# Where a pair's copies out of PSUM stand in the order of a two-layer graph attention kernel

## The chip, the cores and the metric

The kernel runs on one core of a Trainium2 chip. The metric is device time in microseconds (us), the median of several runs; lower is better. Times inside an execution come from one profiled execution.

## What is computed

Two graph attention layers over a batch of 8 graphs with 2048 nodes and 256 features, each followed by a residual add and a layer norm. Layer 0 has 8 heads of 32 features and additive scores; layer 1 has one head and scores from a product.

```python
def _L0_gnn_ref(x, adj, prior, W, a_src, a_dst, beta_tilde, W_out):
    x_proj = jnp.einsum('bnd,hdf->bhnf', x, W)
    e_src = jnp.einsum('bhnf,hf->bhn', x_proj, a_src)
    e_dst = jnp.einsum('bhnf,hf->bhn', x_proj, a_dst)
    e = jax.nn.leaky_relu(e_src[..., :, None] + e_dst[..., None, :], ALPHA)
    e = e + (beta * jnp.log(prior + EPS))[:, None, :, :]
    e = jnp.where(adj[None, None, :, :] > 0, e, neg_inf)
    attn = jax.nn.softmax(e, axis=-1)
    h = jnp.einsum('bhij,bhjf->bhif', attn, x_proj)
    return h.transpose(0, 2, 1, 3).reshape(B, N, D) @ W_out.T
...
def _L1_gnn_ref(inp, adj, W1, W2, W3):
    h1, h2, h3 = inp @ W1, inp @ W2, inp @ W3
    e = jax.nn.leaky_relu(jnp.einsum('bnd,bmd->bnm', h1, h2), ALPHA)
    e = jnp.where(adj[None, :, :] > 0, e, NEG_INF)
    return jax.nn.relu(softmax(e) @ h3)
...
x = _layernorm(x + _L0_gnn_ref(x, adj, adj[None], ...), axis=-1)
x = _layernorm(x + _L1_gnn_ref(x, adj, ...), axis=-1)
```

## The kernel before

**Layer 0** is the class `Gat`, one object per batch. It works on pairs of heads (four pairs, 0 to 3) and on 16 column tiles of 128 nodes per pair; one call of `step` does one tile of one pair, 64 steps per batch. VectorE (DVE) makes two score tiles `s` of 128x2048 (L381, from `c`, `re` and the matrix `mt` loaded from memory; the ring of such tiles has eight). TensorE (PE) multiplies them into two PSUM accumulators, `val` (the weighted sums) and `den` (the denominators), both 128x1024 and with one buffer each (L414). From batch 1 on, for pairs 1 to 3, half or so of the denominators' terms are added up beforehand in two tiles `d`: the first term by ScalarE (ACT, L399), the others by DVE (L394); at the end of the pair one product of `d` with ones adds them into `den`.

When the last tile of a pair is done, `finish` empties the accumulators on ACT: two copies of half of `val` each into `ht` (L429) and one of `den` into `dn` (L431). `finish` is a generator: its further stages, one per later step, are a small load `rc` from `dn`, a reciprocal on DVE (L436), a round trip through memory (`rec_d`, `rb`) and the scaling of `ht` (L457).

**Layer 1** is the class `Dot`, which works on the batch before. One call of its `step` does one row tile of 128 nodes: for each of four column blocks, PE transposes a block of the last row tile's probabilities `p` into a PSUM tile `pt` (L580), ACT copies it to `pts` (L582), PE makes the next row tile's scores `e` for that block (L554) and ACT writes them to `p` (L556). Then PE multiplies `pts` into `acc` (L596), DVE masks the new `p` and takes its extreme (L559, `neg`), ACT takes the exponential (L562), scales `acc` into `z` (L601), and DVE (`z` L602, `st` L226, `mv` L228) and ACT (`f` L230 to L233, `z` L234) normalise the row tile. Every fourth row tile PE first makes new queries `h` (L543), copied by ACT (L545). All the PSUM tiles `pt`, `e`, `h1p` and the like rotate through three buffers of one tag (`mm`).

**The order.** The main loop puts a few steps of layer 0 of batch b between the row tiles of layer 1 of batch b-1. The last step of each pair comes at the end of such a group, so a row tile of `Dot` follows it (after pair 0: the end of `turn` and the start of `Dot`). PE's order, and from the main loop on SP's too, is the order in which the code is written. On the other engines a scheduler orders the instructions, with the order of writing as the priority; each engine then executes its instructions in that fixed order. The generators of finished pairs are kept in the list `later`, which all batches share, and each step of layer 0 advances each of them once.

Of the kernel before, what the change touches and what calls it, by code (L numbers as in the profile page):

```python
# [27 lines left out]
def kernel(  # L28
# [51 lines left out]
    def mm_tile(name):  # L80
        return ps.tile([P, BK], F32, tag="mm", name=name)

    def ring_tile(name, shape=(P, N)):


        return wide.tile(list(shape), F32, tag="s", name=name, bufs=8)

    def wide_tile(name, tag, bufs, dtype=F32):
        return wide.tile([P, N], dtype, tag=tag, name=name, bufs=bufs)
# [116 lines left out]
    def load_mt(jt, tag="mt"):  # L206
        mt = wide_tile("mt", tag, 2)
        nc.sync.dma_start(mt, mt_d[ts(jt, P), :])
        return mt
# [13 lines left out]
    def layer_norm(z):  # L223

        st = small.tile([P, nc.vector.BN_STATS_DIM], F32, name="st", bufs=2)
        nc.vector.bn_stats(st, z)  # L226
        mv = small.tile([P, nc.vector.BN_AGGR_DIM], F32, name="mv", bufs=3)
        nc.vector.bn_aggr(mv, st)  # L228
        f = small.tile([P, 4], F32, name="f", bufs=3)
        nc.scalar.activation(f[:, 0:1], mv[:, 1:2], AF.Ln, bias=eps_ln)  # L230
        nc.scalar.activation(f[:, 1:2], f[:, 0:1], AF.Exp, scale=-0.5)
        nc.scalar.mul(f[:, 2:3], mv[:, 0:1], -1.0)
        nc.scalar.activation(f[:, 3:4], f[:, 1:2], AF.Identity, scale=f[:, 2:3])  # L233
        nc.scalar.activation(z, z, AF.Identity, bias=f[:, 3:4], scale=f[:, 1:2])  # L234

    def row_tile(name, bufs=4):
        return small.tile([P, D], F32, tag="row", name=name, bufs=bufs)


    class Gat:  # L240

# [104 lines left out]
        def step(self, count=1):  # L346

            for _ in range(count):
                hp, jt = next(self.units)
                for work in list(self.later):  # L350
                    if next(work, self) is self:
                        self.later.remove(work)
                if hp == NP - 1 and jt == 0 and self.b + 1 < B:
                    gats[self.b + 1].load_factors()

                at = self.b * NP + hp + 1
                if at < B * NP:
                    gat = gats[at // NP]
                    if jt == 4 and gat.b > 0:
                        gat.load(at % NP)  # L360
                    elif jt == 12:
                        gat.scale(at % NP)
                if jt == 0:
                    if self.b > 0:
                        self.cs = [self.cs_ahead.pop(0) for _ in range(HP)]
                    else:
                        self.cs = [self.query_rows(hp * HP + a) for a in range(HP)]
                    self.val = pacc.tile([P, HALF], F32, tag="val", name="val")
                    self.den = pacc.tile([P, HALF], F32, tag="den", name="den")
                first = self.b == 0 and hp == 0  # L370
                if first:
                    self.more_mt(jt + 2, jt > 0)
                if self.b > 0:
                    mt = self.mts.pop(0)
                else:
                    mt = self.mts[jt] if first else load_mt(jt, ("mt", "d")[jt % 2])
                s = []
                for a in range(HP):
                    h = hp * HP + a
                    sa = ring_tile("s")  # L380
                    nc.vector.scalar_tensor_tensor(sa, self.cs[a], self.re[:, 0, jt, h:h + 1], mt, ALU.max, ALU.mult)  # L381
                    s.append(sa)
                    if self.b > 0 and jt == NT - 1:
                        self.cs_ahead += [c for c in [next(self.c_loads, None)] if c]
                if self.b > 0:
                    ahead = 2 if hp > 0 or not 1 < jt < 10 else min(4, 11 - jt)
                    while len(self.mts) < ahead and (mt := next(self.mt_loads, None)):
                        self.mts.append(mt)
                v, e = self.v[hp], self.re[:, 1]
                heads = [hp * HP + a for a in range(HP)]  # L390
                chain = SUMMED[self.b][hp]
                if jt - 1 in chain[1:]:
                    for d, sa, h in zip(self.sums, self.last, heads):
                        nc.vector.scalar_tensor_tensor(d, sa, e[:, jt - 1, h:h + 1], d, ALU.mult, ALU.add)  # L394
                self.last = s
                if jt in chain[:1]:
                    self.sums = [wide_tile("d", "d", 2) for _ in heads]
                    for d, sa, h in zip(self.sums, s, heads):
                        nc.scalar.activation(d, sa, AF.Copy, scale=e[:, jt, h:h + 1])  # L399
                self.products(self.val, [v[:, jt, ts(a, DH)] for a in range(HP)], s, jt == 0, jt == NT - 1)  # L400
                if jt not in chain:
                    self.products(self.den, [e[:, jt, h:h + 1].to_broadcast([P, DH]) for h in heads], s,
                                  jt == min(set(range(NT)) - set(chain)), not chain and jt == NT - 1)
                if chain and jt == NT - 1:
                    self.products(self.den, [ones] * HP, self.sums, False, True)
                if jt == NT - 1:
                    work = self.finish(hp)
                    next(work)
                    self.later.append(work)

        def products(self, dst, weights, s, start, stop):
            for c in range(HALF // BK):
# [116 lines left out]
    class Dot:  # L529
# [35 lines left out]
        def step(self, fill=lambda k: None):  # L565

            it, p, den = self.at, self.p, self.ahead
            self.at += 1  # L570
            xr = row_tile("x1r")
            nc.sync.dma_start(xr, x1_d[self.b, ts(it, P), :])
            fill(0)

            pts = []

            def turned(g):
                t = mm_tile("pt")
                for k in range(IG):
                    nc.tensor.transpose(t[:, ts(k, P)], p[:, ts(g * IG + k, P)], ident)  # L580
                pt = chunk.tile([P, BK], F32, tag="pt", name="pts", bufs=NB)
                nc.scalar.copy(pt, t)  # L582
                pts.append(pt)

            if it + 1 < NT:
                if (it + 1) % IG == 0:
                    self.queries((it + 1) // IG)
                self.scores(it + 1, turned)
            else:
                for g in range(NB):  # L590
                    turned(g)
            acc = pacc.tile([P, D], F32, tag="acc", name="acc")
            for g in range(NB):
                for k in range(IG):
                    j = g * IG + k
                    nc.tensor.matmul(acc, pts[g][:, ts(k, P)], self.h3[:, j, :], start=(j == 0), stop=(j == NT - 1))  # L596
            fill(1)
            rec = small.tile([P, 1], F32, name="rec1", bufs=2)
            nc.vector.reciprocal(rec, den)
            z = row_tile("z")  # L600
            nc.scalar.activation(z, acc, AF.Relu, scale=rec)  # L601
            nc.vector.tensor_add(z, z, xr)  # L602
            layer_norm(z)
            nc.scalar.dma_start(out[self.b, ts(it, P), :], z)
# [79 lines left out]
    for b in range(1, B + 1):  # L684
        gat, fresh = gats[b - 1], gats[b] if b < B else None
# [71 lines left out]
```

## Time and profile before

| | |
|---|---|
| median of 3 runs | 4280.19 us (4280.04 to 4282.62) |
| the profiled execution | 4279.62 us |
| its span, first to last instruction | 4277.8 us |
| mean granted TensorE clock | 0.997 |
| ACT copies `ht<-val` (L429) | 64, 1.01 us each |
| ACT copies `dn<-den` (L431) | 32, 1.01 us each |
| ACT copies `pts<-pt` (L582) | 512, 0.585 us each |
| ACT `d<-s,re` (L399) | about 2.0 us each |
| DVE `s` (L381) | 1024, 2.34 us each |
| DVE idle for `p` from ACT (L559 after L556) | 254.4 us, 29 times |

A group of the timeline is one row: its start from the start of the span, how long it took from first start to last end, engine, line, operation, the tiles written and read, how many instructions; in brackets the engine's idle time before it and what ended that. An instruction's end overlaps the start of the next one on its engine by about a tenth of a microsecond, so start-to-start distances are what adds up.

### The profile page before, as it was taken

The numbers are of one execution on the slowest core, as the hardware profiler recorded it, in microseconds if no ns is written. First come the engines' busy times: TensorE is split into PE (matmuls) and PEld (weight loads), VectorE is DVE, ScalarE is ACT, GpSimd is POOL, SyncE is SP. The second block draws the span as 40 slices with busy tenths as digits, with TensorE's granted clock in tenths as the row PEclk, the third lists the DMA queues.
The fourth block names the chain that finished last, engine by engine and source line by source line (L and its number), as shares of the span: only waits on it lengthen the run. The fifth ranks groups of instructions, "written<-read, shape, count | busy, mean of one in ns | idle before, by whom it ended". The sixth has DMA issues, their size and how long they took to land.

```text
span 4277.8 us, 59110 instructions
## 1 busy us (share of the span) xinstructions
PE 4163.8 (97%) x24928; PEld 2230.3 (52%) x24928; DVE 3618.3 (85%) x2432; ACT 1609.0 (38%) x3007; POOL 10.3 (0%) x14
## 2 busy tenths in 40 slices
PE   7999999999999999999999999999999999999999
PEld 4444355555555555554555555555545555555766
DVE  6888778998899979999799988999799997998222
ACT  6522133333334333342333323333333323343554
POOL 0000000000000000000000000000000000000000
PEclk9999999999999999999999999999999999999999
DMA  7988656657455555555555474556555565553211
GB/s 239 309 287 321 242 210 219 231 203 247 184 201 192 197 205 188 184 196 214 187 208 185 174 248 153 209 187 210 198 191 182 181 233 182 205 182 134 77 49 41
DMA packets 268458, 843.52 MB, mean 197 GB/s; under 512 B 33184, under 2 KB 166304, under 8 KB 194464
## 3 DMA queue, kind: packets, MB, share of 16 engines
q1 hardware_dynamic: 232352, 806.17, 53.2%
q10 hardware_dynamic: 35840, 33.57, 2.3%
q8 instruction: 195, 3.19, 0.3%
q14 instruction: 71, 0.58, 0.0%
HBM read 763.76 MB, written 75.37 MB: 196 GB/s over the span
## 4 chain that ended last, share of the span: by engine, by line
PE 57%; DVE 27%; issue 8%; DMA 5%; ACT 3%; SPq 0%; DVEq 0%; ACTq 0%; POOL 0%; POOLq 0%
DVE s L381 17%; PE acc L596 13%; PE e L554 12%; PE val L414 11%; PE den L414 9%; DVE d L394 6%; PE pt L580 3%; PE h3p L522 2%; DMA mt<-mt_d 2%; PE proj L274 2%; DVE p L559 2%; PE y L483 2%; PE h1p L543 2%; DMA adj_r<-in_adj_dram 1%; DMA adj_t<-in_adj_dram 1%
## 5 line engine op out<-in xcount | busy, mean ns | idle before, releaser
L381 DVE SCALAR_TENSOR_TENSOR s<-c,re,mt 128x2048 f32<-128x2048 f32 x1024 | 2357.5, 2340 | 195.4 <-PE den L414 59.7
L414 PE MATMUL val<-s,v 128*32 128x512 f32 x8192 | 978.8, 597 | 22.0 <-DVE s L381 21.9
L554 PE MATMUL e<-x1t,h 128*128 128x512 f32 x2048 | 964.6, 595 | 21.6 <-ACT pts L582 18.5
L596 PE MATMUL acc<-h,pts 128*128 128x256 f32 x4096 | 905.0, 379 | 0.0
L596 PEld LDWEIGHTS acc<-h,pts 128*128 128x128 f32 x4096 | 777.8, 190 | 156.4 <-issue 57.4
L414 PE MATMUL den<-s,re 128*32 128x512 f32 x5600 | 683.4, 593 | 0.0
L394 DVE SCALAR_TENSOR_TENSOR d<-s,re,d 128x2048 f32<-128x2048 f32 x282 | 654.0, 2343 | 0.0
L414 PEld LDWEIGHTS val<-s,v 128*32 128x32 f32 x8192 | 252.3, 110 | 599.0 <-issue 530.7
L559 DVE CUSTOM_DVE_ANT_0 p<-p,pen 128x2048 f32<-128x2048 f32 x128 | 292.5, 2285 | 260.5 <-ACT p L556 254.4
L554 PEld LDWEIGHTS e<-x1t,h 128*128 128x128 f32 x2048 | 351.2, 190 | 287.6 <-issue 249.8
L556 ACT ACTIVATE p<-e 128x512 f32<-128x512 f32 x512 | 305.2, 596 | 416.9 <-PE e L554 414.3
L562 ACT ACTIVATE p<-p,neg 128x2048 f32<-128x2048 f32 x128 | 256.5, 2004 | 472.2 <-DVE neg L559 472.2
L414 PEld LDWEIGHTS den<-s,re 128*32 128x32 f32 x5600 | 188.9, 110 | 418.8 <-issue 418.8
L580 PEld LDWEIGHTS pt<-ident,p 128*128 128x128 f32 x2048 | 245.2, 141 | 301.5 <-issue 237.5
L582 ACT COPY pts<-pt 128x512 f32<-128x512 f32 x512 | 297.0, 585 | 228.9 <-PE pt L580 226.2
L580 PE MATMUL pt<-ident,p 128*128 128x128 f32 x2048 | 309.8, 276 | 16.0 <-ACT p L562 8.3
L230 ACT ACTIVATE f<-mv,eps_ln 128x1 f32<-128x1 f32 x128 | 37.9, 296 | 434.8 <-DVE mv L228 434.2
L601 ACT ACTIVATE z<-acc,rec 128x256 f32<-128x256 f32 x128 | 60.0, 469 | 250.7 <-PE acc L596 102.4
L274 PE MATMUL proj<-wp,xt 128*128 128x272 f32 (+1 forms) x512 | 130.7, 400 | 4.7 <-ACT xt L182 3.0
L522 PE MATMUL h3p<-w3s,x1t 128*128 128x256 f32 x512 | 122.6, 383 | 6.4 <-ACT x1t L517 4.7
L483 PE MATMUL y<-wot,ht 128*128 128x256 f32 x512 | 119.0, 385 | 3.5 <-ACT x1t L517 2.1
L276 ACT COPY v<-proj 128x256 f32<-128x256 f32 x128 | 47.2, 374 | 197.2 <-PE proj L274 153.7
(88 smaller groups left out, 1895.4 us busy)
## 6 DMA issues: line engine op xcount, KB each, us to landing
mt<-mt_d SPq DMA_DIRECT2D x496, 1024.0 KB
c<-c_d SPq DMA_DIRECT2D x64, 1024.0 KB
pen<-pen_d SPq DMA_DIRECT2D x112, 512.0 KB
xg<-in_x_dram SPq DMA_DIRECT2D x60, 512.0 KB
adj_t<-in_adj_dram SPq DMA_DIRECT2D x16, 1024.0 KB
mt_d<-mt SPq DMA_DIRECT2D x16, 1024.0 KB
rb<-rec_d SPq DMA_DIRECT2D x128, 128.0 KB
x_d<-ht ACTq DMA_DIRECT2D x64, 256.0 KB
```

What stands on the lines that cost most here:

```text
L274: nc.tensor.matmul(t[:, 0:cols], xt[kc][:, ts(it % IG, P)], wp[:, kc, 0:cols], start=(kc == 0), stop=(kc == KC - 1))
L381: nc.vector.scalar_tensor_tensor(sa, self.cs[a], self.re[:, 0, jt, h:h + 1], mt, ALU.max, ALU.mult)
L394: nc.vector.scalar_tensor_tensor(d, sa, e[:, jt - 1, h:h + 1], d, ALU.mult, ALU.add)
L414: nc.tensor.matmul(dst[ts(q, DH), ts(c, BK)], weights[q % 2], s[q % 2][:, ds(q // 2 * HALF + c * BK, BK)], start=start, stop=stop)
L522: nc.tensor.matmul(t[:, ts(i, D)], x1t[:, kc, ts(2 * (j - lag) + i, P)], w3s[:, kc, :], start=(kc == 0), stop=(kc == KC - 1))
L554: nc.tensor.matmul(t, self.h1[:, kc, ts(it % IG, P)], self.x1t[:, kc, ts(c, BK)], start=(kc == 0), stop=(kc == KC - 1))
L556: nc.scalar.activation(p[:, ts(c, BK)], t, AF.Prelu, alpha=ALPHA)
L559: nc.vector.tensor_tensor_reduce(p, p, pen, -1.0, FMAX, ALU.add, ALU.min, neg)
L562: nc.scalar.activation(p, p, AF.Exp, bias=neg, scale=-1.0, accum_out=den)
L580: nc.tensor.transpose(t[:, ts(k, P)], p[:, ts(g * IG + k, P)], ident)
L582: nc.scalar.copy(pt, t)
L596: nc.tensor.matmul(acc, pts[g][:, ts(k, P)], self.h3[:, j, :], start=(j == 0), stop=(j == NT - 1))
```

## The change

At the end of a pair the generator `finish` is no longer advanced at once to its copies. It goes into a list `evictions`. The function `evict` takes what is in that list, issues the copies, and puts the generator into `later`. It is called at the beginning of each step of layer 0, and in layer 1's row tile after the next row tile's scores have been written and before the product `acc`. For batch 0 it is called right at the pair's end.

```diff
+    evictions = []
+
+    def evict():
+
+        while evictions:
+            gat, work = evictions.pop()
+            next(work)
+            gat.later.append(work)
...
         def step(self, count=1):

             for _ in range(count):
+                evict()
                 hp, jt = next(self.units)
                 for work in list(self.later):
...
                 if jt == NT - 1:
-                    work = self.finish(hp)
-                    next(work)
-                    self.later.append(work)
+                    evictions.append((self, self.finish(hp)))
+                    if self.b == 0:
+                        evict()
...
             else:
                 for g in range(NB):
                     turned(g)
+            evict()
             acc = pacc.tile([P, D], F32, tag="acc", name="acc")
```

## The prediction

> **What bounds the kernel now.** I read the page's engine table first, then who waited for whom on PE, then the timeline of PE, ACT and DVE at the ends of the pairs, and the DVE waits in the stretches between them.
>
> ```profile
> PE 4163.8 (97%) x24928; PEld 2230.3 (52%) x24928; DVE 3618.3 (85%) x2432; ACT 1609.0 (38%) x3007; POOL 10.3 (0%) x14
> ...
> PE val L414 <- DVE s L381: 21.9, 17, 4.4
> PE e L554 <- ACT pts L582: 18.5, 24, 1.9
> PE pt L580 <- ACT p L556: 5.7, 12, 0.8
> PE e L554 <- ACT h L545: 3.1, 6, 0.7
> ```
>
> PE is busy for all but 114 us of 4277.8, so this change cannot win much: only PE's gaps are for sale. The second wait line is the one that the change aims at: 24 times the e product waited for ACT's copy of a transposed tile, 18.5 us in all. 15.3 us of it stand at the ends of pair 1 and pair 2 of batches 1 to 7, one each, found by going through the timeline there. Here is one pair 1 end (batch 3), PE and then ACT (start, duration, instruction, in brackets the idle time before it):
>
> ```profile
> 1706.33 1.88 PE L554 MATMUL e<-x1t,h 128*128 128x512 f32 x4
> 1708.05 0.60 PE L580 MATMUL pt<-ident,p 128*128 128x128 f32 x4
> 1709.79 1.99 PE L554 MATMUL e<-x1t,h 128*128 128x512 f32 x4 [1.14 <-ACT pts L582]
> ...
> 1714.18 0.66 PE L580 MATMUL pt<-ident,p 128*128 128x128 f32 x4 [0.26 <-ACT p L556]
> ...
> 1706.35 2.01 ACT L399 ACTIVATE d<-s,re 128x2048 f32<-128x2048 f32 x1 [1.83 <-DVE s L381]
> 1708.26 0.99 ACT L431 COPY dn<-den 128x1024 f32<-128x1024 f32 x1
> 1709.15 0.58 ACT L582 COPY pts<-pt 128x512 f32<-128x512 f32 x1
> ```
>
> The score tiles use three PSUM buffers, so the second e product needs the buffer of the first pt, and that is free only when ACT has copied it. ACT stands in 1.9 us of d (start to start) and 0.9 us of dn before it. The same at the end of pair 2:
>
> ```profile
> 1837.73 1.98 PE L554 MATMUL e<-x1t,h 128*128 128x512 f32 x4 [0.89 <-ACT pts L582]
> ...
> 1834.15 2.00 ACT L399 ACTIVATE d<-s,re 128x2048 f32<-128x2048 f32 x1 [1.39 <-PE den L414]
> 1836.18 1.01 ACT L431 COPY dn<-den 128x1024 f32<-128x1024 f32 x1
> 1837.09 0.59 ACT L582 COPY pts<-pt 128x512 f32<-128x512 f32 x1
> ```
>
> Pair 0 and pair 3 ends show no such gap. One more thing limits the gain: asked for DVE's waits between 1597 and 1830, the trace names none, and the table by stretches (columns: length, busy PE, PEld, DVE, ACT, POOL, clock, DMA share, GB/s) has DVE at 100% there, while PE still runs almost without gaps:
>
> ```profile
> 1604.00:1704.00 100.00, 98.95 (x583) 52.18 (x582) 100.00 (x62) 31.45 (x58) 0.00 (x0) 1.00 0.50 180
> 1704.00:1724.00 20.00, 18.60 (x86) 11.15 (x90) 20.00 (x16) 12.82 (x20) 0.00 (x0) 1.00 0.77 285
> 1724.00:1834.00 110.00, 109.55 (x664) 56.25 (x656) 107.30 (x72) 37.68 (x74) 0.00 (x0) 1.00 0.51 181
> ```
>
> So in pairs 1 and 2 DVE and PE are level, and PE time won at the end of pair 1 is kept only as far as DVE delivers.
>
> **What the Trainium skill says.** "PSUM — Partial Sum Buffer", section "Engine vs sequencer instructions": the queues of ScalarE and VectorE are strict FIFO. The trace agrees: pt was ready at 1706.99 and its copy waited 2.16 us behind d and dn. "Perfetto Trace Analysis", section "Optimizing Scalar/DVE Operations": an unsaturated Scalar engine can still cause bubbles on other engines. ACT is at 38% here and makes this one. The same page, section "Identifying the Most-Contended Engine", warns that PE's busy share is no measure of distance from its limit; I use only PE's gaps, 98 us between its matmuls (the rest of the 114 is ahead of the first). The prices below are all from the trace.
>
> **The change part by part.** No instruction is added or removed. In the changed program PE's order and SP's and POOL's queues are the same as before, DMAs included. Batch 0 evicts at once as before. What moves, by the order in which the built programs hold their instructions:
>
> (a) ACT, pairs 1 and 2: the two val copies and the first d stay ahead of the first pts copy; dn goes behind the second pts copy. Pair 1, replayed with the start-to-start times above: d 1706.35, pts 1708.26 (done 1708.84), p 1708.74, pts 1709.23, two small f 1709.71, dn 1710.0, p 1711.0. The second e starts at about 1708.9 instead of 1709.79: 0.89 won, 0.25 of the gap stays. p at 1711.0 instead of 1713.54 also ends the 0.26 gap before the last pt, because the second d now stands behind it. Pair 1: 1.15 us.
>
> (b) Pair 2: pts 1836.08, p 1836.57, pts 1837.05, dn 1837.53, d 1838.43, p 1840.33. The second e starts on time (the 0.89 gap goes). But the last pt needs the buffer that this p empties at 1840.93, and now wants it at about 1840.6: a new gap of some 0.35, where before the 0.89 gap had hidden it. After it the next pts copy, 1841.4, is just in time. Net about 0.6 to 0.7 us.
>
> (c) DVE between the ends of pair 1 and pair 2: the scheduler puts p (L559) one s (2.26 us) earlier twice, and one d earlier once, and mv (L228) of one tile ahead of one d. Before, that mv (1779.45) held ACT's f/z chain and the h copy behind it, and PE waited 0.45 us at 1781.74. In the new order mv is some 1.8 us earlier, so this gap goes as well, even with PE 1.15 us earlier. Against it: at 1716.1 DVE now meets p at the head of its queue; ACT finishes writing it at about 1716.55, so DVE idles some 0.45 us in a stretch without slack. At its other early places p has been written 0.8 us before or more.
>
> (d) What is late next: the s of the last row tile of pair 2. Before, it ended at 1827.83 and PE's val product began at 1828.77, 0.93 later (in batches 2 to 7 alike). In the new order z, st and one rec stand behind it (about 0.8 us less), plus 0.45 idle: 1827.5. PE may then start at 1827.5 at the earliest, so of the 1.6 us won in (a) and (c) some 1.3 are kept.
>
> (e) Pair 0: dn moves from before the x1t copy to between the two h copies. ACT had 1.13 us idle before the second h, dn takes 0.9: hidden; without that cover it would cost at most 0.9. The h and dn tiles also swap places in a ring of four; both take places of xg tiles long read. Pair 3: one f between the val copies. Nothing.
>
> (f) rc's load waits for dn, now about 1 to 2 us later. SP is in order, so the mt and rb loads behind it could start later. DVE's rc (L436) comes at 1716.10, 6.9 us after dn's end, so I take nothing; the bounds are 0 and 1 us per end. The den product that overwrites the PSUM of dn comes 15 us later.
>
> Batch 1: its pair 1 gap (1.87 us) ends with pts held by an f that waits for mv at 708.2, and stays; its pair 2 is as (b), but DVE there waits for DMA. I take 0.5 us.
>
> Sum: six batches (2 to 7) by 1.3 + 0.65 = 11.7, plus 0.5: 12.2 us. The profiled execution took 4279.62 us (span 4277.8 and 1.8 around it), 0.57 below the median of 4280.19. 4280.19 - 12.2 is about 4268.
>
> **The rivals.**
> Both ends in full: no cap in (d), no new gap in (b): 6 x (1.40 + 0.45 + 0.89) + 0.5 = 17 us, 4263. For it: the replay's margins are tenths. Against it: DVE at 100%.
> DVE swallows pair 1: only (b) stays, 6 x 0.65 + 0.5 = 4.4, 4276. It happens if DVE loses about 1.3 us more than replayed. For it: no DVE idle time before; against: the new order itself gives 0.8 back.
> The stall only moves: dn, wherever it stands on ACT, delays a p or pts copy that PE needs, the gaps keep their sum, 4280. Against it: ACT idles 1.10 us before the last p of the pair 1 tile, so dn has room there.
> Slower: p at the head of DVE's queue. Each place where p moved forward blocks the s behind it if p is not yet written, and DVE's loss goes one to one to the last s of pair 2. From a loss of about 3.5 us per batch (three places, 1.2 us each) it outweighs all gains; at 5 us per batch 6 x 1.5 = 9 us, 4289. Against it: p was written 0.8 us before two of the three places.
>
> **How the numbers follow.** A difference under 0.2%, 8.6 us, can't be told from none. Chances: the forecast 0.62 (its own spread 4263 to 4272, with 0.02 of it inside the 0.2%), both ends in full 0.15, swallowed 0.12, moved 0.06, slower 0.05. Faster 0.60 + 0.15 = 0.75; same 0.02 + 0.12 + 0.06 = 0.20; slower 0.05. The range 4261 to 4276 leaves out the slower and moved cases and the far end of the best one, under 0.2.
>
> **What would show it.** Right: the wait of e for pts falls from 18.5 us to about 4 to 6; the wait of e for h (3.1 us) falls to almost nothing; a gap of some 0.35 us before the last pt, for p, at pair 2 ends; PE's gap sum falls from 98 to about 86 us; DVE shows its first short idle at p after pair 1. Wrong: PE val waiting for s at the end of pair 2 by a microsecond or more, or DVE idle for p summing to several us per batch.

## The result and the profile after

| | before | after |
|---|---|---|
| median, run side by side | 4280.42 us (4275.43 to 4286.95) | 4268.28 us (4263.92 to 4270.0) |
| ratio, 95% interval | | 0.9969 (0.996 to 0.9978) |
| span of the profiled execution | 4277.8 us | 4267.8 us |

The change saves 12.1 us at the median; the interval of the ratio allows 9.4 to 17.1 us. The two spans differ by only 10.0. In the profiled execution of after, TensorE's granted clock was 0.92 between 1000 and 1045 us, against 1.00 in that of before: by an estimate from these figures 0.08 of 45 us, or 3.6 us, were lost there. Pair 0 of batch 2, in which the stretch lies, took 115.79 us instead of 111.56. The stages below lie outside it.

The engine line of the page of after, and then the waits of PE in it (total us, times, longest):

```profile
PE 4169.3 (98%) x24928; PEld 2234.3 (52%) x24928; DVE 3617.9 (85%) x2432; ACT 1606.5 (38%) x3007; POOL 10.3 (0%) x14
...
PE val L424 <- DVE s L391: 24.1, 17, 4.4
...
PE e L564 <- ACT pts L592: 5.1, 15, 1.3
...
PE pt L590 <- ACT p L566: 3.5, 6, 0.6
```

The wait of `e` for `pts` fell from 18.5 to 5.1 us. The wait of `e` for `h` (3.1 us before) is no longer among PE's waits. All idle time between matmuls, summed over the records, fell from 98.0 to 82.3 us.

The end of pair 1 in batch 3, in the timeline of after, PE and then ACT. The instructions sit about 2.7 us later in this execution than in that of before, so only distances compare:

```profile
1709.03 1.88 PE L564 MATMUL e<-x1t,h 128*128 128x512 f32 x4
1710.74 0.60 PE L590 MATMUL pt<-ident,p 128*128 128x128 f32 x4
1711.57 1.98 PE L564 MATMUL e<-x1t,h 128*128 128x512 f32 x4 [0.23 <-ACT pts L592]
...
1709.05 2.00 ACT L409 ACTIVATE d<-s,re 128x2048 f32<-128x2048 f32 x1 [1.83 <-DVE s L391]
1710.95 0.56 ACT L592 COPY pts<-pt 128x512 f32<-128x512 f32 x1
...
1712.66 1.02 ACT L441 COPY dn<-den 128x1024 f32<-128x1024 f32 x1
```

`dn` now stands 1.71 us behind the first `pts` copy instead of 0.89 ahead of it. The gap before the second `e` is 0.23 instead of 1.14 us, and the gap before the last `pt` is gone.

The end of pair 2 in the same batch: DVE, ACT, PE.

```profile
1827.05 2.35 DVE L391 SCALAR_TENSOR_TENSOR s<-c,re,mt 128x2048 f32<-128x2048 f32 x1
1829.31 0.22 DVE L610 RECIPROCAL rec<-den 128x1 f32<-128x1 f32 x2
...
1829.55 0.47 ACT L612 ACTIVATE z<-acc,rec 128x256 f32<-128x256 f32 x1 [4.82 <-issue]
...
1833.09 2.03 ACT L439 COPY ht<-val 64x1024 f32<-64x1024 f32 x2 [0.41 <-PE den L424]
1835.02 2.00 ACT L409 ACTIVATE d<-s,re 128x2048 f32<-128x2048 f32 x1
1837.05 0.58 ACT L592 COPY pts<-pt 128x512 f32<-128x512 f32 x1
...
1838.48 1.04 ACT L441 COPY dn<-den 128x1024 f32<-128x1024 f32 x1
...
1835.22 1.88 PE L564 MATMUL e<-x1t,h 128*128 128x512 f32 x4
1836.94 0.60 PE L590 MATMUL pt<-ident,p 128*128 128x128 f32 x4
1837.68 1.98 PE L564 MATMUL e<-x1t,h 128*128 128x512 f32 x4
```

`dn` has moved here too, but ACT came late to its `val` copies. VectorE now takes the reciprocal `rec` of a row tile behind the last `s` of the pair, so ACT's `z` could not start before 1829.55, and the layer norm's chain held ACT until its `out` transfer was issued. The page names PE as what ended the 0.41 us before the copies, but ACT was issuing that transfer then. The second `e` still comes late.

**Where the time went.** Below, a "tile" is one of layer 0's 16 column tiles (the expectations sometimes say row tile), and each stage is the distance between the starts of two tiles' `val` products on PE, taken from the records. In batches 2 to 7 of after, nearly every stage repeats within some hundredths of a microsecond. Before is less even: B ranges from 73.86 to 74.17, and A is 0.3 and 0.6 us longer than usual in two batches. Even so, stages tell apart what medians can't. Typical values:

| stage | before | after | change |
|---|---|---|---|
| A: tile 15 of pair 1 to tile 0 of pair 2 | 24.14 | 22.63 | -1.51 |
| B: tiles 0 to 9 of pair 2 | 73.96 | 73.25 | -0.71 |
| C: tiles 9 to 15 of pair 2 | 31.29 | 31.48 | +0.19 |
| D: tile 15 of pair 2 to tile 0 of pair 3 | 22.10 | 21.82 | -0.28 |
| tile 0 to tile 15 of pair 3 | 104.54 | 104.54 | 0 |
| tile 15 of pair 3 to tile 15 of pair 0 | 114.67 | 114.67 | 0 |
| E: tile 15 of pair 0 to tile 15 of pair 1 | 125.24 | 125.24 | 0 |

That is 2.3 us per batch. Over four whole batches (tile 15 of pair 1, batch 3 to batch 7) the distance fell from 1985.96 to 1975.52 us, 2.6 per batch; the rest is mostly in before's longer A and B.

### The profile page after: what moved, and what is told of

It reads as the page before. It is cut to its first block, busy times and chain, and to the rows that moved or that the text cites. A ratio compares the mean times of both kernels' runs of the same rounds, so it can differ in the third digit from the quotient of the medians.

```text
span 4267.8 us, 59104 instructions
## 1 busy us (share of the span) xinstructions
PE 4169.3 (98%) x24928; PEld 2234.3 (52%) x24928; DVE 3617.9 (85%) x2432; ACT 1606.5 (38%) x3007; POOL 10.3 (0%) x14
## 4 chain that ended last, share of the span: by engine, by line
PE 57%; DVE 26%; issue 8%; DMA 4%; ACT 4%; SPq 0%; DVEq 0%; POOL 0%; ACTq 0%; POOLq 0%
DVE s L391 16%; PE acc L607 13%; PE e L564 12%; PE val L424 12%; PE den L424 8%; DVE d L404 5%; PE pt L590 3%; DMA mt<-mt_d 2%; PE h3p L532 2%; PE proj L283 2%; PE h1p L553 2%; DVE p L569 2%; PE y L493 1%; ACT d L409 1%; DMA adj_r<-in_adj_dram 1%
```

## The experiments

Twelve kernels were run, in four groups; before was run beside each group (4278.63 to 4282.13 us). The stages are those of the profiled execution, batch 3 unless said otherwise.

**1. Each engine's new order alone.** The edit in the source moves ACT's copies; that VectorE's order changes as well is the scheduler's doing. In these two kernels an engine's order was fixed by orderings that wait on nothing:

```diff
+    for a, b in zip(order, order[1:]):
+        tc.add_manual_dep(mine[b], mine[a].name, DependencyInfo(NoSync, DATA))
 e1: source of after,  ScalarE in the order of after,  VectorE in the order of before
 e2: source of before, ScalarE in the order of before, VectorE in the order of after
```

> The changed kernel with VectorE's instructions held in the order of the kernel before; ScalarE in the order of the changed kernel. Theory A (the two orders are needed together): the gap before the second e product at the end of pair 1 falls from 1.14 to about 0.23 us, but the 1.1 us won are lost again some 70 us later, where e waits for the copy of h behind f and z, which wait for VectorE's mv: that gap grows from 0.45 to about 1.6 us. Pair 2 keeps about 0.4 us. Total gain 2 to 4 us; the distance between the same product in batch 3 and batch 7 falls from 1986.0 us to about 1984. Theory B (the place of dn on ScalarE alone makes the gain): 10 us or more, distance about 1976.

> The kernel before with VectorE's instructions in the order that they have in the changed kernel; ScalarE in the order of the kernel before, dn in front. Theory A: the gaps of 1.14 at the end of pair 1 and 0.89 at the end of pair 2 stay, the 0.45 wait for h goes, and some 0.3 are lost at the row tile after pair 2, where f and z come later. Gain 1 to 3 us, distance from batch 3 to 7 about 1984. Theory B: no gain (within 1 us).

| | A | B | C | D | ratio (interval) |
|---|---|---|---|---|---|
| e1, ScalarE alone | 22.63 | 75.49 | 31.29 | 21.62 | 0.9991 (0.9985 to 0.9998) |
| e2, VectorE alone | 24.14 | 73.61 | 31.29 | 22.10 | 0.9991 (0.9983 to 1.0) |
| both: after | 22.63 | 73.25 | 31.48 | 21.82 | 0.9969 (0.996 to 0.9978) |

Each order alone saves about 4 us at the median (4274.95 and 4276.27 against 4279.78), and for VectorE's the interval reaches no change. Over the four whole batches the two save 3.3 and 2.9 us (1982.63 and 1983.03 against 1985.96), where both together save 10.4: more than the sum. With ScalarE's order alone, stage A is won in full and stage B gives all of it back. The reason is visible in where VectorE takes `p` of the row tile at the end of pair 1. These are VectorE's rows there: before, then e2, then after.

```profile
1716.36 2.25 DVE L381 SCALAR_TENSOR_TENSOR s<-c,re,mt 128x2048 f32<-128x2048 f32 x1
1718.53 2.28 DVE L559 CUSTOM_DVE_ANT_0 p<-p,pen 128x2048 f32<-128x2048 f32 x1
```

```profile
1712.60 6.94 DVE L381 SCALAR_TENSOR_TENSOR s<-c,re,mt 128x2048 f32<-128x2048 f32 x3
1720.62 2.29 DVE L559 CUSTOM_DVE_ANT_0 p<-p,pen 128x2048 f32<-128x2048 f32 x1 [1.08 <-ACT p L556]
```

```profile
1712.02 6.86 DVE L391 SCALAR_TENSOR_TENSOR s<-c,re,mt 128x2048 f32<-128x2048 f32 x3
1718.81 2.29 DVE L569 CUSTOM_DVE_ANT_0 p<-p,pen 128x2048 f32<-128x2048 f32 x1
```

Before, `p` stands behind another `rc` and `s` on VectorE, however early ACT has written it. In e2 it stands ahead of that `s`, but ACT hasn't written it, and VectorE idles 1.08 us. Only with both orders is `p` both written and next in line. From this `p` on VectorE has no idle time above 0.02 us in after up to tile 15 of pair 2. The stretch behind it then follows from when `p` starts, as the starts in the profiled executions show (us, batch 3):

| kernel | tile 15 of pair 1 to `p` on VectorE | `p` to tile 15 of pair 2 | sum = A + B + C |
|---|---|---|---|
| before | 19.15 | 110.24 | 129.39 |
| e1, ScalarE's order alone | 19.15 | 110.26 | 129.41 |
| e2, VectorE's order alone | 17.97 | 111.07 | 129.05 |
| after | 16.73 | 110.63 | 127.37 |
| e3, e5 (below) | 16.93, 16.92 | 110.63, 110.62 | 127.56, 127.54 |
| e8 (below) | 17.78 | 110.63 | 128.41 |

The second column is 110.62 or 110.63 us in after, e3, e5 and e8 alike, although `p` comes between 16.73 and 17.78 us after tile 15. What stages A to C gain is what `p` gains: 2.42 us, less 0.39 for the new order behind it. This is the bound that VectorE sets. TensorE's own work sets another: in batches 2 to 7 no run has a B below 73.25 or a C below 31.29. After stands at 73.25 and 31.48, so a still earlier `p` could win no more than 0.19 us in B and C.

**2. Each pair alone.**

```diff
-                    if self.b == 0:
+                    if self.b == 0 or hp != 1:      # e3: only pair 1 deferred
+                    if self.b == 0 or hp != 2:      # e4: only pair 2 deferred
                         evict()
```

> Only pair 1's copies are written late; pairs 0, 2 and 3 evict at once. The scheduler then makes nearly the whole new VectorE order by itself. Theory A: most of the gain, 9 to 12 us, since pair 2's own part is worth almost nothing in the changed kernel; the gap at the end of pair 2 stays at about 1 us. Theory B: the share of pair 1 in the removed dn waits, 6 x 1.15 = 7 us.

> Only pair 2's copies are written late. VectorE's order differs from the kernel before in one place per batch alone (an s ahead of mv in the row tile after pair 2). Theory A: of the 0.89 us at the end of pair 2 some 0.35 come back as a wait of the last pt for p and 0.3 as a wait for pts in the next row tile: gain 0 to 2 us. Theory B: 6 x 0.65 = 4 us.

With pair 1 alone: 4268.35 us, 0.9973 (0.9961 to 0.9984), A 22.63 (22.91 in one batch), B 73.25 to 73.55, C 31.48 to 31.50, D 22.30. With pair 2 alone: 4275.24 us, 0.999 (0.9983 to 0.9997), A to C as before, D 21.62. In the undisturbed batches of e3 the stages fall by 1.83 us, in e4 by 0.48, and together that is the 2.31 of after. So four fifths of the gain come from pair 1, whose row tile feeds that `p`; pair 2 alone saves more than I had expected of it.

**3. What is left, and what `dn` costs at each place.** In e5 the first scaled copy `d` goes behind the first `pts` as well; in e6 VectorE's last additions to pair 2's sums nearly vanish, so that most of that pair's denominators lack tile 14; e7 and e8 make `dn` twice, in before and in after. VectorE's order is fixed in all four, ScalarE's apart from the edit.

```diff
 e5, ScalarE, batches 2 to 7
-pair 1: ht ht z d pts p pts              pair 2: ht ht d pts p pts dn d p pts p pts p
+pair 1: ht ht z pts d p pts              pair 2: ht ht pts d p pts dn p pts d p pts p
 e6
+                        w = DH if self.b > 1 and hp == 2 and jt == NT - 1 else N
-                        nc.vector.scalar_tensor_tensor(d, sa, e[:, jt - 1, h:h + 1], d, ALU.mult, ALU.add)
+                        nc.vector.scalar_tensor_tensor(d[:, 0:w], sa[:, 0:w], e[:, jt - 1, h:h + 1], d[:, 0:w], ALU.mult, ALU.add)
 e7 (before), e8 (after)
             nc.scalar.copy(dn, self.den)
+            if b > 1 and hp in (1, 2):
+                nc.scalar.copy(dn, self.den)
```

> The kernel after with VectorE's order kept and ScalarE's order changed in two places of each of the batches 2 to 7: at the end of pair 1 and of pair 2 the first scaled copy d (2.00 us) goes behind the first copy pts, and at pair 2 the second d goes behind the second Prelu copy p. Theory A (what is left of the stall is ScalarE's queue: pts waits behind d): the gap of 0.23 us before the second e of pair 1 goes and with it 0.5 us of stage A (22.63 to 22.1), the two gaps of pair 2 (0.145 and 0.135 us) go and with them 0.7 us of stage D (21.82 to 21.1); 6 x 1.2 = 7 us, 4261 us (4259 to 4264). Rival (VectorE, which delivers the last s just when TensorE wants it, takes back whatever TensorE wins in pair 1): only D shrinks, 6 x 0.7 = 4 us, 4264 us, and stage C grows by what stage A won.

> The kernel after with the orders of ScalarE and VectorE kept; in pair 2 of batches 2 to 7 VectorE's last two additions to the sums (row tile 14, 2.3 us each, just ahead of the last s) run over 64 of 2048 columns, so row tile 14 is left out of most of that pair's denominators. VectorE is 4.5 us ahead at the end of pair 2. If step (d) of the prediction holds (the last s sets when the pair's last product can start, and row tile 2's gains beyond it are lost): stage C falls from 31.48 to 31.2 or below, and since p, z and the layer norm come earlier too, stage D falls by up to 0.4; 6 x 0.3 to 0.7 = 2 to 4 us, 4264 to 4266 us. If the last s is just in time by accident and holds nothing up: C stays at 31.48, D within 0.1 of 21.82, 4268 us.

> The kernel before with the orders of ScalarE and VectorE kept and the copy dn (1.01 us) made twice in pairs 1 and 2 of batches 2 to 7, the second right behind the first, where it stands ahead of the first copy pts. Theory A (the copies ahead of pts are on the path with their whole length): stages A and D grow by 0.9 to 1.05 us each, 6 x 1.9 = 11.5 us, 4291 us (4288 to 4294). Rival (what ended the stall was the orders' interaction, and the length of dn is mostly hidden): under 4 us, 4280 to 4284 us.

> The kernel after with the orders of ScalarE and VectorE kept and dn made twice in pairs 1 and 2 of batches 2 to 7, behind the first copies pts, where the changed kernel has it. Theory A (behind pts the copy lies beside TensorE's products): stages A and D grow by less than 0.3 us each, 4268 to 4271 us. Rival (the copy has moved its wait to the later copies p and pts of the same row tile): 0.5 us or more each, 4274 us or more, with gaps before the third and fourth pt.

| | A | B | C | D | median | ratio (interval) |
|---|---|---|---|---|---|---|
| e5, `d` behind `pts` | 22.13 | 73.91 | 31.50 | 20.97 | 4266.75 | 0.9967 (0.9954 to 0.9979) |
| e6, last sums left out (batch 2) | 22.63 | 73.25 | 31.49 | 21.62 | 4262.56 | 0.9958 (0.9944 to 0.9971) |
| e7, `dn` twice in before (batch 6) | 25.18 | 73.87 | 31.29 | 23.14 | 4296.49 | 1.0036 (1.0023 to 1.005) |
| e8, `dn` twice in after | 22.78 | 74.14 | 31.49 | 22.88 | 4280.67 | 0.9995 (0.9987 to 1.0004) |

e5: the gaps at both pair ends went, and A and D fell by 0.50 and 0.85 us, as its first theory said. But B took back 0.66, and the median lies above both forecasts (4261 and 4264). VectorE reached its `p` no sooner (16.92 against 16.73), and the wait of `e` for `h` came back in pair 2:

```profile
1778.90 0.16 DVE L228 BATCH_NORM_AGGREGATE mv<-st 128x2 f32<-128x6 f32 x1
...
1780.62 0.34 ACTq L615 DMA_DIRECT2D out_dram<-z  x1
1781.00 1.07 ACT L555 COPY h<-h1p 128x512 f32<-128x512 f32 x2 [0.41 <-PE h1p L553]
...
1781.64 1.98 PE L564 MATMUL e<-x1t,h 128*128 128x512 f32 x4 [0.24 <-ACT h L555]
```

This timeline shows how VectorE sets PE's pace without any `p` or `s` being waited for: `mv`, the end of a layer norm's statistics, comes late on VectorE; ACT, in order, runs `f`, `z` and the `out` transfer behind it, and only then the copy `h` that PE needs. The rival of this run was right that VectorE takes back what TensorE wins in pair 1, and wrong about the place and the instruction (it had named the last `s` and stage C). In C the same thing costs the 0.19 us, here in after:

```profile
1806.67 0.17 DVE L228 BATCH_NORM_AGGREGATE mv<-st 128x2 f32<-128x6 f32 x1
...
1808.40 0.34 ACTq L615 DMA_DIRECT2D out_dram<-z  x1
1808.78 0.59 ACT L592 COPY pts<-pt 128x512 f32<-128x512 f32 x1 [0.41 <-ACT z L234]
1808.89 0.60 PE L590 MATMUL pt<-ident,p 128*128 128x128 f32 x4
...
1809.42 1.98 PE L564 MATMUL e<-x1t,h 128*128 128x512 f32 x4
```

PE shows no idle time here, as `pt` is recorded to 1809.49, yet `e` starts 0.53 us after it instead of the usual 0.43 to 0.44, and runs 0.10 us longer.

e6 (its short additions run over 32 columns, not the 64 of the expectation): the last `s` started 2.5 us earlier against tile 15's product (4.91 us ahead of it instead of 2.40), and stage C did not move: 31.49. So the last `s` was not what held pair 2's end in after. That it came just 0.04 us ahead of PE fits `mv` setting PE's time and VectorE's order setting the distance from that `mv` to `s`. D lost 0.20: `rec` comes early again, and the second `e` starts 0.58 us after its `pt` instead of 0.74. The median of e6 lies below that of after, but the intervals overlap, and the stages account for 1.2 us of it.

e7: doubling `dn` where it stands ahead of `pts` costs 1.04 us each in A and D in the quiet batches (up to 2.7 in others), and 14.4 us at the median against the 11.5 expected. e8: behind `pts` the same copy costs stage A 0.15, but stage B 0.89 and stage D 1.06. Here the theory missed, and its rival was right about pair 2. In all the second copy costs 2.1 us per batch behind `pts`, and 2.0 ahead of it in the quiet batches of e7: behind `pts` there is room for one copy, not for two. In pair 2, that room was used up; PE, and for pair 1 VectorE, in the timeline of e8:

```profile
1847.21 0.66 PE L592 MATMUL pt<-ident,p 128*128 128x128 f32 x4 [1.19 <-ACT p L568]
```

```profile
1723.00 2.29 DVE L571 CUSTOM_DVE_ANT_0 p<-p,pen 128x2048 f32<-128x2048 f32 x1 [0.98 <-ACT p L568]
```

In pair 1, PE did have the room, but ACT finished the row tile's last `p` later, VectorE idled 0.98 us with `p` at the head of its queue, and tile 15 of pair 2 came 1.04 us later (128.41 against 127.37).

**4. `mv` right behind its `st`.** If `mv` is what ties PE to VectorE in pair 2, it can be moved ahead of the 2.3 us instruction that VectorE's order puts between the two. The edit is on VectorE's order alone: e9 on before, e10 on e1, e11 on e5; e12 is e11 without the three moves of pair 1 in each of the batches 2 to 7.

```diff
-VectorE: s st d mv d s
+VectorE: s st mv d d s
```

> The kernel before with both orders kept, except that on VectorE each mv goes right behind its st (61 of 128 move, by one s, d or pen). Theory M (the wait of e for h in pair 2 is the wait for mv: mv behind a d of 2.3 us, then f, z and the out transfer on ScalarE, then the copy h): the gap of 0.45 us goes and stage B falls from 74.0 to 73.25, A, C and D stay at 24.14, 31.29 and 22.10; 6 x 0.75 = 4.5 us, 4276 us. Rival (the gap follows VectorE's total work, which is unchanged): B stays within 0.2 of 74.0, 4280 us.

> ScalarE in the order of after, VectorE in that of before, as in the run with ScalarE's order alone, and each mv right behind its st. Theory M: what took stage A's gain away there (B 75.49) was mv behind long VectorE instructions, so B falls to 73.25 to 73.6 while A 22.63, C 31.29 and D 21.62 stay; A to D 148.8 to 149.2 against 149.2 of after: 4266 to 4269 us, as good as both new orders together. Rival (VectorE's whole order of s, p and d is needed): B stays above 74.5, 4272 to 4275 us.

> The run with the copies d behind pts (A 22.13, B 73.91, C 31.49, D 20.97), and each mv right behind its st. Theory M: B returns to 73.25 and C to 31.29, A and D stay, A to D 147.6 to 147.7 against 149.2 of after; 6 x 1.5 = 9 us, 4259 us (4257 to 4262), the fastest of all. Rival (VectorE has no idle time between the end of pair 1 and the last s of pair 2, so nothing won in A can be kept): B stays at 73.9, 4265 us.

> The run with the copies d behind pts and every mv early, but in the batches 2 to 7 the three mv of pair 1 (row tiles 6, 9 and 13) stay where after has them. Theory S (a point where VectorE has no slack gains nothing from an earlier TensorE, and every stop costs TensorE more than its length: with every mv early TensorE came to the end of pair 1 1.3 us sooner and lost 1.7 there): A returns to 22.13 and the stretch of pair 1 to 125.24, together 147.4 instead of 147.8; B stays 73.25, C 31.29; D between 20.97 (no wait left) and 22.4 (the wait for the last s of pair 2 as before). From pair 1 of batch 3 to that of batch 7 1971 to 1975 us instead of 1975.7; 4254 to 4261 us. Rival (VectorE's work between the two pair ends is the bound, wherever its mv stand): the same distance as there within 1 us, 4260 to 4262 us, and D grows by what B and C win.

| | E | A | B | C | D | median | ratio (interval) |
|---|---|---|---|---|---|---|---|
| e9 | 123.93 | 25.86 | 73.25 | 31.29 | 22.60 | 4275.01 | 0.9994 (0.9986 to 1.0002) |
| e10 | 123.94 | 24.35 | 73.67 | 31.29 | 23.22 | 4271.80 | 0.9982 (0.9974 to 0.9989) |
| e11 | 123.93 | 23.86 | 73.25 | 31.29 | 22.38 | 4260.80 | 0.9952 (0.994 to 0.9965) |
| e12 | 125.24 | 22.14 | 73.25 | 31.29 | 22.38 | 4257.64 | 0.995 (0.9937 to 0.9964) |

B falls to 73.25 where only `mv` has moved (e9 against before, e11 against e5), and C to 31.29 in e11: that wait was `mv`. In e10, where `p` keeps its old place behind `rc` and `s`, B falls from 75.49 to 73.67: what PE feels in B is not `p` itself but the `mv` behind it. But A and D did not stay, against all three expectations. With `mv` early in pair 1, PE reaches tile 15 of pair 1 1.31 us sooner, finds VectorE not ready (in e9 it waits 0.78 us for `s` and 0.88 for `d`), and loses 1.72. So moving `mv` alone wins next to nothing: from batch 3 to batch 7 e9 takes 1984.89 us, before 1985.96. e12, with the moves in pair 1 undone, has A and E as in e5. At the end of pair 2 PE now really runs into the last `s`. In e12, DVE and PE:

```profile
1814.34 2.35 DVE L391 SCALAR_TENSOR_TENSOR s<-c,re,mt 128x2048 f32<-128x2048 f32 x1
...
1816.74 1.49 PE L424 MATMUL val<-s,v 128*32 128x512 f32 x11 [0.40 <-DVE s L391]
```

D is 1.41 us longer than in e5, so it takes back the 0.66 of B and the 0.21 of C and more: e12's expectation had both ends in it, and the upper one came. From batch 3 to batch 7 e12 takes 1974.43 us, e11 1975.67, e5 1974.55 and after 1975.52, so by the stages e12 is no better than e5. Its profiled execution is ahead of that of after by 13.4 us at tile 15 of pair 1 in batch 3 (1688.64 against 1702.07). Of these, 4.8 us lie ahead of the first tile of batch 1, which starts anywhere between 468.1 and 474.6 us in the fourteen profiled executions, and 6.0 in pair 0 of batch 2, where after had the lower clock; in e11 and e12 the clock was 1.00 there. So most of the lower medians of e11 and e12 is not shown to come from `mv`. e12 has the lowest median, 0.5% under before, but its interval overlaps those of e11, e6 and e5, and just that of after.

## Why the prediction came out right, step by step

The direction and the main mechanism were right: `dn` ahead of `pts` held PE's second `e`, and VectorE limits what of that gain is kept. That the sum, 12.2 us, met the measured 12.1 to a tenth is luck. The measurement allows 9.4 to 17.1 us, and the stages of the six batches add up to 6 x 2.31 = 13.9. Of the terms, pair 1 with the wait for `h` was forecast too small (1.3 us kept, 2.03 measured) and pair 2 too large (0.65, against 0.28), which cancel in part.

- (a) Pair 1, predicted 1.15, measured 1.51 in stage A. The mechanism is as replayed: the gap of 1.14 became 0.23. The first `pts` copy had waited longer than the prediction says, 2.66 us and not 2.16, as the `pt` before it ended at 1706.49; the replay does not use that figure. What was too small is the price of the last gap: 0.26 us recorded, 0.59 lost by start-to-start distances (1711.61 to 1714.18 to 1716.51 in before, 2.57 + 2.33 against twice 2.155).
- (b) Pair 2, predicted 0.6 to 0.7, measured 0.28. The replay left the `val` copies and the start of `d` at before's times, and took `d` as 1.93 us from start to start where its own lines have 2.03 (1834.15 to 1836.18). It missed that `rec`, behind the last `s` in the new order (step (d) even names it there), holds `z` and so the `val` copies: they start 3.65 us after tile 15's `val` product instead of 1.96. `d` comes 0.20 and `pts` 0.30 us later than replayed (1837.05 - 1829.44 = 7.61 against 1836.08 - 1828.77 = 7.31): 0.20 by `rec`, 0.10 by the length of `d`. The replay had nothing to spare, so the second `e` still loses 0.42 us. e4 and e6, where `rec` is early, have a D of 21.62 instead of 21.82. The new gap before the last `pt` came as forecast; it is recorded as 0.135 instead of 0.35 us but costs 0.44. Before, the gap of 0.89 had cost 1.16: 1.16 - 0.42 - 0.44 = 0.30.
- (c) The wait of `e` for `h` went, as forecast, by an earlier `mv`. It was worth 0.71, not the 0.45 of the recorded gap. These are the lines of before, ahead of the `e` that waits:

```profile
1779.45 0.16 DVE L228 BATCH_NORM_AGGREGATE mv<-st 128x2 f32<-128x6 f32 x1
...
1782.19 1.98 PE L554 MATMUL e<-x1t,h 128*128 128x512 f32 x4 [0.45 <-ACT h L545]
```

The forecast idle 0.45 us of VectorE at `p` did not come: the three `s` ended just as ACT had written `p` (written at 1718.77, taken at 1718.81). That `p` comes 2.42 us earlier on VectorE is what lets pair 1's gain be kept in after, by way of the `mv` behind it; the prediction counted the earlier `mv`, but saw in the earlier `p` mainly a danger.
- (d) The cap. The last `s` ended 127.32 us after tile 15 of pair 1, against 128.45 before; the forecast 1827.5 would be 128.1. PE gained 2.03 us up to tile 15 of pair 2, not 1.3. That VectorE limits what is kept was right; that it does so through the last `s` was wrong for after (e6) and right one step further (e12). In after it does so through `mv`, and only by the 0.19 us in C.
- (e), (f) Nothing at pairs 0 and 3 and nothing by `rc`: the typical stages there are equal to 0.01 us. Whether batch 1 gained the forecast 0.5 us can't be told. From its tile 15 of pair 0 to the start of batch 2 before takes 415.16 us and after 414.39, but e7 and e6, whose edits leave batch 1 alone, take 414.54 and 415.18.
- A slip without effect on the sum: of PE's 114 us outside its busy time, 98 lie between matmuls, as it says, but the rest is not all ahead of the first one; 10.1 us are, and 6.0 come behind the last.

Of the rivals, the one in which VectorE swallows pair 1 is what ScalarE's order alone does (e1: A -1.51, B +1.53). The slower one, `p` at the head of VectorE's queue, is a mechanism at work in e2 (1.08 us idle) and e8 (0.98); in e8 its price went to the end of pair 2 almost one to one. In after it has just no effect, by a margin of 0.04 us: in e5, with `d` behind `pts`, VectorE idles 0.12 us and `p` comes 0.19 us later. "The stall only moves" holds with a second `dn` (e8). That e7 costs what it does shows that the copies ahead of `pts` lay on PE's path with their whole length.

## What to carry to other kernels

Where two engines are level, follow not the instruction that was moved but the first one behind it on the saturated engine: here one `p` on VectorE, behind which the next 110 us follow as long as VectorE has no idle time. A source edit that moves one engine's work lets the scheduler reorder the others; fix the orders one at a time before crediting the edit, since neither may be worth much alone. When a stall has gone and the time hasn't, look for a short instruction (here 0.18 us of statistics) behind a long one on the saturated engine, at the head of a chain that an in-order queue puts before a copy. Then look at what comes next: moving it removed its wait, but the time went to the next place where VectorE was not ready (e9, e12).

## What the hardware showed unexpectedly

- A recorded gap between matmuls understates its cost. `e` normally starts 0.43 to 0.44 us after `pt` begins, though `pt` is recorded as 0.60 long, and the first `e` after a wait lasts 1.98 instead of 1.88. So the gap of 1.14 us cost 1.40, that of 0.23 cost 0.50, and a wait of 0.1 us that leaves no gap at all cost 0.19. On the narrow `val` products it is more: e12's stage D, with the 0.40 as its only recorded gap, is 1.41 us longer than that of e5.
- Many stages repeat within 0.02 us between batches and between kernels (E is 123.93 to 123.94 or 125.23 to 125.25 in batches 2 to 7 of all fourteen), while whole runs of one kernel spread over 3 to 12 us. Effects of 0.2 us per batch that no median could show are plain in them.
